# Partial softmax sums on VectorE in the first four attention units of a decoder layer

## The chip, the cores and the metric

The kernel runs on one NeuronCore of one Trainium2 chip, in fp32 throughout. The metric is the device time of one execution in microseconds. Five engines run side by side and are joined by semaphores: TensorE (PE; its weight loads are listed apart as PEld), VectorE (DVE), ScalarE (ACT), GpSimd (POOL) and the transfer queue of SyncE (SP). Matmul results go to PSUM banks of 128 partitions by 512 fp32 values.

## The reference, cut to what matters

A pre-norm decoder layer over 4 batches of 1024 tokens of width 512, with three residual blocks:

```
x = x + attn(layernorm(x))            # gated attention, 16 heads of 32
x = x + xattn(layernorm(x), ctx)      # cross attention, 16 heads of 32, 1024 context tokens
x = x + ffn(layernorm(x))             # 512 -> 64, 16 relu units for each of the 64, -> 512
```

The first attention divides twice, which is why two sums are needed:

```
attn_align = softmax(alignment)                                  # over keys
attn = attn_align * aperture[query] * expression[key]
attn = attn / (attn.sum(over keys) + 1e-8)
converged = attn @ v
```

With e = exp(score), the quotient needs the plain sum of e over the keys and the gated sum of e times expression[key], for each query and head. The cross attention needs the plain sum alone.

## The kernel before, in words

The work is cut into eight *units*: units 0 to 3 are the first attention of batches 0 to 3, units 4 to 7 the cross attention. A unit has two *halves* (512 queries each), a half has four *groups* of four heads, and a group runs over eight *key tiles* of 128 keys. One key tile of one group is a *step* (`attention`, `step`); there are 512. I call one group of one half of one unit a *group half*, written (unit, half, group).

A step does this:

- `scores` (L631): TensorE multiplies keys by queries for the four heads into two PSUM tiles `s`, each two banks wide. ScalarE turns each into a tile `e` of two heads by 512 queries (L637). There are six buffers of `e`, and a step takes two: `es[0]` holds the first two heads of the group, `es[1]` the third and fourth.
- Then VectorE adds. In units 0 to 3 it adds the first two heads up over the key tiles, plainly (L659 and L661, tile `es`) and with the gates (L668 on ScalarE begins it at key tile 1, L669 on VectorE goes on, tile `eg`).
- One step later, `times` (L684): TensorE multiplies `e` by the values into `av`. For the third and fourth heads it also makes the sums: after each odd key tile a *round* of four matmuls (L694) takes two key tiles times two heads; its weights are two columns of `sw`, a column of ones and the gates, so one matmul gives plain and gated sum, accumulated over the group in PSUM `sm`. A group half of units 0 to 3 has four such rounds.
- At the end of a group, `normalize` copies `av` and `sm` out (ScalarE, L703 and L705). One step on, after the scores of step 1 of the next group, `add_up` sums `es` and `eg` over the 128 partitions with matmuls by ones (L716), ScalarE copies the result (L717), small transfers rearrange the sums, and some steps later `divide` (L740 to L760) and `multiply` (L767) on VectorE apply the reciprocals to `q`, where `av` was put.

In units 4 to 6 VectorE adds all four heads. In the last unit the third and fourth heads of most groups go to TensorE by rounds of ones; there `added_up` names runs of three key tiles that VectorE adds up first.

Beside the steps, `run` deals out other work in proportion to its cost: projections of the next unit into two banks `f` (`bank`; L107), emptied by VectorE (`v` of units 0 to 3 L557, output projections L861) or ScalarE (L309, L311); layer norms on VectorE and GpSimd; the small feed-forward network of the previous half in units 5 to 7 (`hidden`, L1013 to L1024, in tiles `hid` with five buffers; `outputs`, L1035 and L1043). The order of work on every engine is the order in which the program issues it; nothing is reordered.

The output weights `wout` and output bias `bout_bc` of the network are constants that GpSimd's queue loads early (`load_networks` in unit 1, `load_biases` before unit 0). After the last step a hand-written tail (`go`) finishes the last half: the output products of the held half before it (`held_out`), transposes (`tr`), the network's inputs (`inputs`), hidden units and outputs.

Of the kernel before, what the change touches and what calls it, by code (L numbers as in the profile page):

```python
# [69 lines left out]
def moderate_path(tc: tile.TileContext, a: dict, out: bass.AP, flag: bass.AP):  # L70
    nc = tc.nc
    x = a["x"]
    with ExitStack() as st:
# [51 lines left out]
        make_identity(nc, ident)  # L125
        fixed = const.tile([P, 3], F32, name="fixed")
        ones, share, power = (fixed[:, i : i + 1] for i in range(3))
        for one, is_ in ((ones, 1.0), (power, -0.5), (share, 1.0 / M)):
            nc.gpsimd.memset(one, is_)

# [103 lines left out]
        bout_bc = const.tile([P, D], F32, name="bout_bc")  # L234

        def load_biases():

            nc.gpsimd.tensor_copy(bqk[:, 0, :], S[0]["rs"])
            for k in range(2):
                nc.gpsimd.dma_start(  # L240
                    bqk[k * 2 * DH : (k + 1) * 2 * DH], a["bqk"].rearrange("p w (c k) -> p w c k", k=2)[:, :, :, k]
                )
            nc.gpsimd.dma_start(bvT, a["xattn_bv"].rearrange("(c p) -> p c", p=P))
            nc.gpsimd.dma_start(bo_bc, a["xattn_bo"].partition_broadcast(P))
            nc.gpsimd.dma_start(bout_bc, a["ffn_bout"].partition_broadcast(P))
            by_quarters([nc.gpsimd.dma_start], win, a["ffn_Win"])

        def fold_bv(part=[]):
# [12 lines left out]


        win = const.tile([P, NC, M], F32, name="win")
        wout = const.tile([P, D], F32, name="wout")
        fb = const.tile([P, 4], F32, name="fb")
        units = const.tile([P, 4, INNER], F32, name="units")
        per = P // INNER

        def load_networks(k):
            r = slice(k * M, (k + 1) * M)  # L270
            nc.gpsimd.dma_start(wout[r, :], a["ffn_Wout"])
            nc.gpsimd.dma_start(fb[r, 0:2], a["ffb"])
            for c in range(NF):
                for w in range(3):
                    nc.gpsimd.dma_start(
                        units[k * M + c * per : k * M + (c + 1) * per, w, :],
                        a["units"].rearrange("(m h) w c -> c w m h", h=INNER)[c, w],
                    )
        def fold_bin():

            nc.vector.scalar_tensor_tensor(
                units[:, 1, :], units[:, 0, :], fb[:, 0:1], units[:, 1, :], ALU.mult, ALU.add
            )
            nc.vector.tensor_tensor(units[:, 3, :], units[:, 1, :], units[:, 2, :], ALU.mult)
            nc.vector.tensor_reduce(fb[:, 2:3], units[:, 3, :], AX.X, ALU.add)
            nc.vector.tensor_reduce(fb[:, 3:4], units[:, 3, 0:EARLY], AX.X, ALU.add)
            for i in (2, 3):
                nc.vector.tensor_tensor(fb[:, i : i + 1], fb[:, i : i + 1], fb[:, 1:2], ALU.add)
            nc.vector.tensor_scalar(units[:, 3, :], units[:, 1, :], -1.0, None, ALU.mult)
# [87 lines left out]
        def pre(u):  # L377
# [119 lines left out]
            def gates(hf):  # L497
                def f():

                    pg = bank()  # L500
                    for c in range(NC):
                        for t in range(4):
                            nc.tensor.matmul(  # L503
                                pg[t * 2 * H : (t + 1) * 2 * H, 0:P], lhsT=wae[:, c, :],
                                rhs=me["in", hf, "t"](c, t), start=(c == 0), stop=(c == NC - 1),
                            )

                    gi = p2.tile([P, 2 * P], F32, tag="hid", name="gi", bufs=5)[:, 0:P]
# [96 lines left out]
        def attention(u, hf):  # L605
# [6 lines left out]
            def shared(g):  # L612
                return ph == 0 or (u + 1 == len(order) and not (g == 1))

            added_up = {(0, 0): (0, 4), (0, 2): (0,), (0, HG - 1): (0, 4), (1, 0): (0, 4), (1, 2): (0,)} if u + 1 == len(order) else {}

            def apart(g):
                return 2 if u + 1 < len(order) else 3
# [1 line left out]
            def closing(g):  # L620
                return (u, hf, g) == (len(order) - 1, 1, HG - 1)

            def scores(g, kt):
# [38 lines left out]
                if ph == 0 and kt > 0:  # L662
                    if kt == 1:
                        me["eg"] = p1.tile([P, 2, HALF], F32, tag="es1", name="eg")
                    for h in range(2):
                        eg, gate = me["eg"][:, h, :], lambda t: me["sw"][:, t, HG * g + h, 1:2]
                        if kt == 1:
                            nc.scalar.activation(eg, me["e", 0][0][:, h, :], AF.Identity, scale=gate(0))  # L668
                        nc.vector.scalar_tensor_tensor(eg, es[0][:, h, :], gate(kt), eg, ALU.mult, ALU.add)  # L669
                return es  # L670

            def by_ones(tiles, first, last):
# [8 lines left out]
            def times(g, kt, es):  # L681
                for h in range(HG):
                    r = slice(h * DH, (h + 1) * DH)
                    nc.tensor.matmul(  # L684
                        av[r, :], lhsT=me["v"][:, kt, HG * g + h, :], rhs=es[h // 2][:, h % 2, :],
                        start=(kt == 0), stop=(kt == NT - 1),
                    )
                own = added_up.get((hf, g), ())
                if shared(g) and kt % 2 and kt - 1 not in own and not closing(g):

                    for j in range(4):
                        t, h = kt - 1 + j // 2, j % 2
                        rhs = me["es"][1] if t - 2 in own else me["e", t][1]
                        nc.tensor.matmul(  # L694
                            sm[j * DH : j * DH + sums, :],
                            lhsT=me["sw"][:, t, HG * g + 2 + h, :] if ph == 0 else ones, rhs=rhs[:, h, :],
                            start=(kt == (3 if 0 in own else 1)), stop=(kt == NT - 1),
                        )

            def normalize(g):  # L700
                i = (u * 2 + hf) * HG + g
# [115 lines left out]
        def post(u, hf):  # L817
# [76 lines left out]
                nc.vector.scalar_tensor_tensor(nm, res["mv"][:, 0:2, 0], -1.0, res["rs all"], ALU.mult, ALU.mult)  # L894

            def more_bias(t):
                return lambda: nc.gpsimd.tensor_tensor(res[t], res[t], bout_bc, ALU.add)

            def prepare():
                all_ = p2.tile([P, NC, T], F32, tag="k", name="rest")  # L900
# [34 lines left out]
                back(rows_d[b][hf], res["xn"])  # L935

            def biased(t):
                return lambda: nc.vector.tensor_tensor(res[t], res[t], bout_bc, ALU.add)

            def tr(t):  # L940
                def f():
# [63 lines left out]
            def hidden(h):  # L1005
                def f():
# [1 line left out]
                    part = (u, hf) == (n - 2, 0)  # L1008
                    own = u + 1 < n and (h < EARLY or not part)
                    if h < INNER:  # L1010
                        hid = p2.tile([P, 2 * P], F32, tag="hid", name="hid", bufs=5)
                    if own and h < INNER:
                        nc.vector.tensor_scalar(  # L1013
                            hid, res["s"], units[:, 0, h : h + 1], units[:, 3, h : h + 1], ALU.mult, ALU.max
# [16 lines left out]
            def outputs(t):  # L1031
                def products():
                    po = res["po", t] = [behind(), behind()] if u + 1 == n else [bank(), bank()]
                    for k in range(2):
                        nc.tensor.matmul(  # L1035
                            po[k], lhsT=res["g"][k * M : (k + 1) * M, ts(t, P)], rhs=wout[k * M : (k + 1) * M, :],
                            start=True, stop=True,
                        )
# [12 lines left out]
                return f, products, add  # L1051
# [64 lines left out]
        def one(f):  # L1116
            return [[(0, f)]]
# [13 lines left out]
        def beside(u, hf):  # L1131
# [768 lines left out]
```

## Time and profile before

| | |
|---|---|
| median of 3 runs | 2150.87 us (2150.67 to 2151.63) |
| profiled execution, its own time | 2150.95 us |
| its span, first to last instruction | 2149.2 us |
| granted TensorE clock | 0.999 |
| busy: TensorE, VectorE, ScalarE, GpSimd | 2132.1, 1529.4, 1234.8, 136.3 us |
| attention steps, first `av` to the tail | 103.7 to about 2112 us |
| units 0 to 3 | 103.7 to 1194.1 us |

How to read the rows: a row of the page's groups has line, engine, operation, output<-input by tile names, shapes, count, then busy time in us and mean length in ns, then the engine's idle time just before these instructions and what ended it. An fp32 matmul of the program shows as two records, so a round of four matmuls has eight. Matmuls overlap: the length of a record or run reaches into the next, and what a round takes of TensorE is read from start to start. A row of the timeline has start and length in us, then the same names; equal neighbours are merged, and brackets give the engine's idle time before and who ended it. A row of the windows has the stretch, its length, busy time of each engine with counts, the granted clock, the share of the transfer engines and GB/s.

### The profile page before, as it was taken

To read this page: it belongs to the slowest core of one execution; us is meant where nothing else is said; L and a number is where in the kernel's file an instruction comes from. 1 tells how busy PE (TensorE), PEld (TensorE's weight loads), DVE (VectorE), ACT (ScalarE), POOL (GpSimd) and SP (SyncE) were. 2 spreads that over 40 slices of the span, in tenths; PEclk is the share of its full clock that TensorE was granted. 3 is DMA by queue.
4 is the path that set the end of the run, shared out by engine and by line. 5 is a ranking of instruction groups with operands and counts; after the bars stand their busy time and mean duration, and the time that the engine had idled before them with its cause. 6 is when DMAs were issued, how large, how long until landed. Compare 5 with 4: busy or idle time off the path is not lost.

```text
span 2149.2 us, 52523 instructions
## 1 busy us (share of the span) xinstructions
PE 2132.1 (99%) x22556; PEld 549.5 (26%) x22556; DVE 1529.4 (71%) x2275; ACT 1234.8 (57%) x1499; POOL 136.3 (6%) x182
## 2 busy tenths in 40 slices
PE   9999999999999999999999999999999999999997
PEld 4322222222222222222222222222222222222223
DVE  3477575687666875657567576787778778788887
ACT  0156545655556554565656666565656656577774
POOL 2000010040030100001000010000000000000001
PEclk9999999999999999999999999999999999999999
DMA  6412133132341312212322213231433223232231
GB/s 165 129 47 56 65 99 111 21 90 72 81 117 31 86 39 71 71 42 72 67 74 74 67 46 70 77 104 47 109 86 80 78 54 71 71 90 71 71 91 50
DMA packets 154496, 161.81 MB, mean 75 GB/s; under 512 B 47366, under 2 KB 93062, under 8 KB 153100
## 3 DMA queue, kind: packets, MB, share of 16 engines
q1 hardware_dynamic: 150188, 156.26, 26.2%
q8 instruction: 179, 2.93, 0.6%
q0 software_dynamic: 2080, 0.98, 0.3%
q10 hardware_dynamic: 1984, 1.12, 0.2%
q14 instruction: 65, 0.53, 0.1%
HBM read 115.53 MB, written 42.73 MB: 74 GB/s over the span
## 4 chain that ended last, share of the span: by engine, by line
PE 96%; DVE 2%; ACT 1%; issue 1%; DMA 0%; POOL 0%; SPq 0%; DVEq 0%; POOLq 0%; ACTq 0%
PE f L107 37%; PE s L631 24%; PE av L684 22%; PE sm L694 6%; PE sm L716 3%; PE f L960 1%; ACT e L637 1%; PE s L107 1%; DVE es L661 1%; PE f L631 1%; PE f L1035 0%; DVE res L1043 0%; DMA xin<-in_x 0%; PE f L503 0%; PE f L994 0%
## 5 line engine op out<-in xcount | busy, mean ns | idle before, releaser
L637 ACT ACTIVATE e<-s 128x1024 f32<-128x1024 f32 x999 | 971.4, 1023 | 704.6 <-PE s L631 495.0
L661 DVE TENSOR_TENSOR es<-es,e 128x1024 f32<-128x1024 f32 x542 | 650.0, 1224 | 244.3 <-ACT e L637 243.2
L631 PE MATMUL s<-q,k 32*64 32x512 f32 x7992 | 585.9, 613 | 0.4 <-ACT e L637 0.2
L684 PE MATMUL av<-e,v 128*32 128x512 f32 x4096 | 548.0, 603 | 0.0
L107 PE MATMUL f<-xT,w 128*32 128x512 f32 x2816 | 333.7, 592 | 0.0
L669 DVE SCALAR_TENSOR_TENSOR eg<-e,sw,eg 128x512 f32<-128x512 f32 x448 | 315.3, 745 | 9.0 <-ACT eg L668 9.0
L659 DVE TENSOR_TENSOR es<-e 128x1024 f32<-128x1024 f32 x97 | 115.9, 1222 | 209.8 <-ACT e L637 199.4
L107 PE MATMUL f<-w,q 128*32 128x512 f32 x1984 | 238.3, 592 | 1.8 <-DVE q L767 1.7
L631 PEld LDWEIGHTS s<-q,k 32*64 32x64 f32 x7992 | 127.7, 129 | 413.8 <-ACT e L637 203.3
L684 PEld LDWEIGHTS av<-e,v 128*32 128x32 f32 x4096 | 87.6, 108 | 403.1 <-issue 402.8
L107 PEld LDWEIGHTS f<-xT,w 128*32 128x32 f32 x2816 | 92.0, 110 | 210.6 <-issue 207.6
L694 PE MATMUL sm<-e,sw 128*2 128x512 f32 x1024 | 133.3, 592 | 0.0
L107 PE MATMUL f<-w,xT 128*32 128x512 f32 x896 | 106.0, 592 | 0.6 <-DVE q L313 0.6
L107 PEld LDWEIGHTS f<-w,q 128*32 128x32 f32 x1984 | 64.3, 110 | 152.4 <-issue 143.0
L107 PE MATMUL f<-w,ctxT 128*32 128x512 f32 x768 | 92.3, 592 | 0.0
L107 PE MATMUL f<-ctxT,w 128*32 128x512 f32 x768 | 92.3, 592 | 0.0
L869 POOL TENSOR_TENSOR r<-res,bo_bc 128x512 f32<-128x512 f32 x32 | 40.9, 1280 | 760.2 <-DVE res L861 634.6
L716 PE MATMUL sm<-es,fixed 128*1 128x512 f32 x356 | 65.0, 591 | 0.0
L319 POOL TENSOR_SCALAR rs<-fmv 128x4 f32<-128x4 f32 (+2 forms) x18 | 11.8, 657 | 835.8 <-DVE fmv L866 835.5
L861 DVE TENSOR_TENSOR res<-f,res 128x512 f32<-128x512 f32 x62 | 42.4, 684 | 19.6 <-PE f L107 12.1
L1024 DVE SCALAR_TENSOR_TENSOR g<-hid,units,g 128x256 f32<-128x256 f32 x105 | 50.1, 477 | 2.7 <-ACT hid L1017 1.9
L767 DVE TENSOR_TENSOR q<-q,recb 128x512 f32<-128x512 f32 x63 | 43.0, 683 | 6.3 <-DMA recb<-rec_d 6.2
(283 smaller groups left out, 1167.1 us busy)
## 6 DMA issues: line engine op xcount, KB each, us to landing
recb<-rec_d SPq DMA_DIRECT2D x252, 64.0 KB
xT<-rows_d SPq DMA_DIRECT2D x60, 256.0 KB
rows_d<-r SPq DMA_DIRECT2D x60, 256.0 KB
w<-in_xattn_Wo SPq DMA_DIRECT2D x9, 1024.0 KB
w<-wout_d SPq DMA_DIRECT2D x8, 1024.0 KB
res<-in_x SPq DMA_DIRECT2D x32, 256.0 KB
x1b_d<-r SPq DMA_DIRECT2D x32, 256.0 KB
res<-x1b_d SPq DMA_DIRECT2D x32, 256.0 KB
```

Source lines behind the costliest of these rows:

```text
L107: nc.tensor.matmul(to[r], lhsT=lhsT[:, j, :] if len(lhsT.shape) == 3 else lhsT[:, r], rhs=rhs, **flags)
L631: nc.tensor.matmul(two[j][m : m + 64], lhsT=k[r, g, kt * P + m : kt * P + m + 64], rhs=q[r, g, :], start=True, stop=True,)
L637: nc.scalar.activation(e[:, h, :] if len(reads) == 1 else e[:, h.start, :], s, AF.Exp, scale=SCALE)
L659: nc.vector.tensor_tensor(me["es"][i], me["e", begin][i], es[i], ALU.add)
L661: nc.vector.tensor_tensor(me["es"][i], me["es"][i], es[i], ALU.add)
L669: nc.vector.scalar_tensor_tensor(eg, es[0][:, h, :], gate(kt), eg, ALU.mult, ALU.add)
L684: nc.tensor.matmul(av[r, :], lhsT=me["v"][:, kt, HG * g + h, :], rhs=es[h // 2][:, h % 2, :], start=(kt == 0), stop=(kt == NT - 1),)
L694: nc.tensor.matmul(sm[j * DH : j * DH + sums, :], lhsT=me["sw"][:, t, HG * g + 2 + h, :] if ph == 0 else ones, rhs=rhs[:, h, :], start=(kt ...
L716: nc.tensor.matmul(sm[j * DH : j * DH + 1, :], lhsT=ones, rhs=e, start=True, stop=True)
L767: nc.vector.tensor_tensor(own, own, all_, ALU.mult)
L861: nc.vector.tensor_tensor(r, res["po"], r, ALU.add)
L1024: nc.vector.scalar_tensor_tensor(res["g"], res["hid"], units[:, 2, h - 1 : h], res["g"], ALU.mult, ALU.add)
```

## The change

In 19 of the 32 group halves of units 0 to 3, VectorE adds up the third and fourth heads over the first m key tiles (m is 4 or 6), plainly into a tile `ep` and with the gates into a tile `et`. ScalarE begins `et` at key tile 1. TensorE's rounds for these key tiles are left out (two or three of four), and one round comes instead, after key tile 6 (m=4) or 7 (m=6), whose four matmuls sum the two heads of `ep` and of `et` over the partitions; `pick` puts the plain sums in the first and the gated sums in the second row. Group halves with m=4: (0,1,0), (0,1,1), (0,1,2), (1,0,0), (1,1,0), (1,1,1), (1,1,2), (2,0,0), (2,1,1), (2,1,2), (3,0,0), (3,0,3), (3,1,0), (3,1,1), (3,1,3). With m=6: (0,1,3), (1,1,3), (2,1,0), (2,1,3).

Room for the two tiles (one buffer each) is made by the constants of the network's output and by `hid`: weights and bias are now loaded in unit 4 into the place of `ep`, and four `hid` buffers are a ring in the place of `et`. The gates get two buffers of their own. In the last unit, (7,1,0) has one run of three key tiles added up in place of two. In the tail, the two output products of the held half stand ahead of the transposes.

```diff
+        pick = const.tile([P, 3], F32, name="pick")
+        nc.gpsimd.memset(pick, 0.0)
+        nc.gpsimd.memset(pick[:, 1:2], 1.0)
...
-            nc.gpsimd.dma_start(bout_bc, a["ffn_bout"].partition_broadcast(P))
...
-            nc.gpsimd.dma_start(wout[r, :], a["ffn_Wout"])
...
+        def load_outs():
+            both = p1.tile([P, 2, HALF], F32, tag="exa", name="outs")
+            outs["w"], outs["b"] = both[:, 0, :], both[:, 1, :]
+            for k in range(2):
+                nc.gpsimd.dma_start(outs["w"][k * M : (k + 1) * M, :], a["ffn_Wout"])
+            nc.gpsimd.dma_start(outs["b"], a["ffn_bout"].partition_broadcast(P))
...
-                    gi = p2.tile([P, 2 * P], F32, tag="hid", name="gi", bufs=5)[:, 0:P]
+                    gi = p2.tile([P, P], F32, tag="gi", name="gi")
...
-            added_up = {(0, 0): (0, 4), (0, 2): (0,), (0, HG - 1): (0, 4), (1, 0): (0, 4), (1, 2): (0,)} if u + 1 == len(order) else {}
+            added_up = {(0, 0): (0, 4), (0, 2): (0,), (0, HG - 1): (0, 4), (1, 0): (0,), (1, 2): (0,)} if u + 1 == len(order) else {}
+
+            gated = {(0, 1, 0): 4, (0, 1, 1): 4, (0, 1, 2): 4, (0, 1, 3): 6, (1, 0, 0): 4, (1, 1, 0): 4, (1, 1, 1): 4, (1, 1, 2): 4, (1, 1, 3): 6, (2, 0, 0): 4, (2, 1, 0): 6, (2, 1, 1): 4, (2, 1, 2): 4, (2, 1, 3): 6, (3, 0, 0): 4, (3, 0, 3): 4, (3, 1, 0): 4, (3, 1, 1): 4, (3, 1, 3): 4}
...
+                m = gated.get((u, hf, g), 0)
+                if 0 < kt < m:
+                    gate = lambda t, h: me["sw"][:, t, HG * g + 2 + h, 1:2]
+                    if kt == 1:
+                        me["ep"], me["et"] = (p1.tile([P, 2, HALF], F32, tag=k, name=k) for k in ("exa", "exb"))
+                        nc.vector.tensor_tensor(me["ep"], me["e", 0][1], es[1], ALU.add)
+                    else:
+                        nc.vector.tensor_tensor(me["ep"], me["ep"], es[1], ALU.add)
+                    for h in range(2):
+                        et = me["et"][:, h, :]
+                        if kt == 1:
+                            nc.scalar.activation(et, me["e", 0][1][:, h, :], AF.Identity, scale=gate(0, h))
+                        nc.vector.scalar_tensor_tensor(et, es[1][:, h, :], gate(kt, h), et, ALU.mult, ALU.add)
...
-                if shared(g) and kt % 2 and kt - 1 not in own and not closing(g):
...
+                if not shared(g) or closing(g):
+                    return
+                own, m = added_up.get((hf, g), ()), gated.get((u, hf, g), 0)
+
+                def round_(seats, start, stop):
+                    for j, (lhsT, rhs) in enumerate(seats):
+                        nc.tensor.matmul(sm[j * DH : j * DH + sums, :], lhsT=lhsT, rhs=rhs, start=start, stop=stop)
+
+                if kt % 2 and kt - 1 not in own and kt >= m:
+                    seats = []
                     for j in range(4):
                         t, h = kt - 1 + j // 2, j % 2
                         rhs = me["es"][1] if t - 2 in own else me["e", t][1]
...
+                        seats.append((me["sw"][:, t, HG * g + 2 + h, :] if ph == 0 else ones, rhs[:, h, :]))
+                    round_(seats, kt == (3 if 0 in own else max(m + 1, 1)), kt == NT - 1 and m < 6)
+                if m and kt == min(m + 2, NT - 1):
+                    seats = [(pick[:, 1 - w : 3 - w], me["et" if w else "ep"][:, h, :]) for w in range(2) for h in range(2)]
+                    round_(seats, False, m == 6)
...
-                        hid = p2.tile([P, 2 * P], F32, tag="hid", name="hid", bufs=5)
+                        if "ring" not in S:
+                            S["ring"], S["turn"] = p1.tile([P, 4, 2 * P], F32, tag="exb", name="ring"), 0
+                        hid = S["ring"][:, S["turn"] % 4, :]
+                        S["turn"] += 1
...
-                return out + k[1] + xT[0] + v[1][0:2] + tr[0]
+                return out + k[1] + xT[0] + v[1][0:2] + (one(load_outs) if u == B else []) + tr[0]
...
-        go(norm[2], bias[2], o[7], lambda: root(3, 1), *tr[0:3], held_out[0][1], look, lambda: within(0, most), norm[3])
-        go(bias[3], *bias[0:2], tr[3], held_out[0][2], lambda: inputs(((0, 0, 2), (1, 2, 1))), held_out[1][1])
-        go(lambda: inputs(((1, 3, 1),)), held_out[1][2], lambda: within(most, most + 1))
+        go(norm[2], bias[2], o[7], lambda: root(3, 1), held_out[0][1], held_out[1][1], *tr[0:3], look, lambda: within(0, most))
+        go(norm[3], bias[3], *bias[0:2], tr[3], held_out[0][2], lambda: inputs(((0, 0, 2), (1, 2, 1))))
+        go(lambda: inputs(((1, 3, 1),)), held_out[1][2], lambda: within(most, most + 1))
```

More of the change, by code (lines that the diff above doesn't have):

```diff
@@ L233, in moderate_path @@
         bo_bc = const.tile([P, D], F32, name="bo_bc")
-        bout_bc = const.tile([P, D], F32, name="bout_bc")
+        outs = {}
         def load_biases():
@@ L263, in moderate_path @@
         win = const.tile([P, NC, M], F32, name="win")
-        wout = const.tile([P, D], F32, name="wout")
         fb = const.tile([P, 4], F32, name="fb")
@@ L687, in times @@
                     )
-                own = added_up.get((hf, g), ())
-                if shared(g) and kt % 2 and kt - 1 not in own and not closing(g):
+                if not shared(g) or closing(g):
[6 more added lines that the diff above has]
+                    seats = []
                     for j in range(4):
@@ L693, in times @@
                         rhs = me["es"][1] if t - 2 in own else me["e", t][1]
[L694 to L698, printed above, removed]
+                        seats.append((me["sw"][:, t, HG * g + 2 + h, :] if ph == 0 else ones, rhs[:, h, :]))
[3 more added lines that the diff above has]
+                    round_(seats, False, m == 6)
             def normalize(g):
@@ L896, in more_bias @@
             def more_bias(t):
-                return lambda: nc.gpsimd.tensor_tensor(res[t], res[t], bout_bc, ALU.add)
+                return lambda: nc.gpsimd.tensor_tensor(res[t], res[t], outs["b"], ALU.add)
             def prepare():
@@ L937, in biased @@
             def biased(t):
-                return lambda: nc.vector.tensor_tensor(res[t], res[t], bout_bc, ALU.add)
+                return lambda: nc.vector.tensor_tensor(res[t], res[t], outs["b"], ALU.add)
             def tr(t):
@@ L1035, in products @@
                         nc.tensor.matmul(
-                            po[k], lhsT=res["g"][k * M : (k + 1) * M, ts(t, P)], rhs=wout[k * M : (k + 1) * M, :],
+                            po[k], lhsT=res["g"][k * M : (k + 1) * M, ts(t, P)], rhs=outs["w"][k * M : (k + 1) * M, :],
                             start=True, stop=True,
```

## The prediction

> **What bounds the kernel now.** I name a group half (u, h, g): unit u, query half h, head group g; each has eight steps, one per key tile. I read first the busy shares and the chain on the page, then the cost of each line, then the timeline of one group half, then windows over the 19 group halves that the change touches.
>
> The page's busy times, the chain by engine, and the lines whose work is moved:
>
> ```profile
> PE 2132.1 (99%) x22556; PEld 549.5 (26%) x22556; DVE 1529.4 (71%) x2275; ACT 1234.8 (57%) x1499; POOL 136.3 (6%) x182
> PE 96%; DVE 2%; ACT 1%; issue 1%; DMA 0%; POOL 0%; SPq 0%; DVEq 0%; POOLq 0%; ACTq 0%
> L661 DVE TENSOR_TENSOR es<-es,e 128x1024 f32<-128x1024 f32 x542 | 650.0, 1224 | 244.3 <-ACT e L637 243.2
> L631 PE MATMUL s<-q,k 32*64 32x512 f32 x7992 | 585.9, 613 | 0.4 <-ACT e L637 0.2
> L669 DVE SCALAR_TENSOR_TENSOR eg<-e,sw,eg 128x512 f32<-128x512 f32 x448 | 315.3, 745 | 9.0 <-ACT eg L668 9.0
> L694 PE MATMUL sm<-e,sw 128*2 128x512 f32 x1024 | 133.3, 592 | 0.0
> ```
>
> TensorE never waits here: 0.4 us ahead of all the score matmuls, 0.0 ahead of the sum matmuls. VectorE waits 243 us for exponentials. So the time is the length of TensorE's stream, as long as nobody makes it wait.
>
> The timeline of group half (0,1,3), start and length in us:
>
> ```profile
> 344.37 1.11 PE L631 MATMUL s<-q,k 32*64 32x512 f32 x16
> 345.42 1.07 PE L684 MATMUL av<-e,v 128*32 128x512 f32 x8
> 346.30 1.04 PE L694 MATMUL sm<-e,sw 128*2 128x512 f32 x8
> 346.58 1.23 DVE L661 TENSOR_TENSOR es<-es,e 128x1024 f32<-128x1024 f32 x1 [1.60 <-ACT e L637]
> 347.16 2.76 PE L107 MATMUL f<-xT,w 128*32 128x512 f32 x24
> 352.11 1.22 DVE L661 TENSOR_TENSOR es<-es,e 128x1024 f32<-128x1024 f32 x1 [1.04 <-ACT e L637]
> 353.25 1.41 DVE L669 SCALAR_TENSOR_TENSOR eg<-e,sw,eg 128x512 f32<-128x512 f32 x2
> 361.34 1.22 DVE L661 TENSOR_TENSOR es<-es,e 128x1024 f32<-128x1024 f32 x1 [2.97 <-ACT e L637]
> 371.71 1.41 DVE L669 SCALAR_TENSOR_TENSOR eg<-e,sw,eg 128x512 f32<-128x512 f32 x2
> 377.74 0.60 PE L716 MATMUL sm<-eg,fixed 128*1 128x512 f32 x2
> ```
>
> Two things are to be seen. A round of four sum matmuls (8 records) takes TensorE from 346.30 to 347.16: 0.86 us; the 1.04 is its length with the overlap into the next round. And VectorE's wide add occupies it from 352.11 to 353.25, 1.14 us, though its length is 1.22; a pair of gated adds takes 1.33 by the same reading (316.38 to 317.71 in the timeline further up).
>
> Windows over the two fullest group halves and the sum over all 19 (length, then busy PE, PEld, DVE, ACT, POOL):
>
> ```profile
> 341.70:378.60 36.90, 36.90 (x391) 9.11 (x387) 21.93 (x32) 21.03 (x27) 0.23 (x1) 1.00 0.56 153
> 618.50:655.40 36.90, 36.90 (x388) 9.11 (x384) 22.77 (x39) 21.02 (x27) 0.23 (x1) 1.00 0.56 153
> sum 677.60, PE 677.60 PEld 167.47 DVE 423.70 ACT 381.04 POOL 39.88; mean PE 35.66 PEld 8.81 DVE 22.30 ACT 20.05 POOL 2.10
> ```
>
> TensorE is busy all the time in them; VectorE has 254 us free.
>
> **The change part by part.**
>
> *TensorE loses rounds.* With m key tiles added up first, m/2 rounds go and one round on the sums comes: 15 group halves with m=4 lose one, 4 with m=6 lose two: 23 rounds, 23 x 0.86 = 19.8 us. The new round has the same shape (two-column weights, 512 columns), so the same price. This lies wholly on the path.
>
> *VectorE gains adds.* Each of m-1 key tiles costs 1.14 + 1.33 = 2.47 us by starts; 15x3 + 4x5 = 65 key tiles are 160.6 us against 254 us free. The slowest rows bound it: a wide add beside GpSimd's took 1.45, and with two gated adds of 0.75 that is 2.95. I take 2.47, the undisturbed row. [...]
>
> Who waits behind these adds? (a) The sum of the gated first two heads, read by the ones-matmuls (L716) in step 1 of the next group. In (0,1,3) VectorE waits 1.60, 0.83, 1.04, 1.16, 2.97, 0.56 and 0.57 us between its first and last add: 8.73 us of cover for 5 x 2.47 = 12.35. The last gated add, which ends at 373.12, ends 3.62 later, at 376.74. Its reader, at 377.72, stands 1.72 earlier (three rounds gone, one come), at 376.00: TensorE waits 0.74, with hand-over some 0.9. (1,1,3) has the same gaps within 0.1: 0.9 again. The same sum over the other seventeen, with what is carried in, leaves the reader 1.1 us or more, least in (2,0,0). (b) Exponentials three steps later need the buffer of e (six buffers, two a step). The smallest margin is 0.2 us, at key tile 3 of (2,0,0), and ScalarE may be 1.7 us late there before scores wait. (c) VectorE's emptying of projection banks (L557, L861): the next use of the bank comes 6 to 7 us after it in these halves, the adds push it by up to 6, and 1.3 us stay. (d) The new round itself runs two steps or more after the last add it reads: 2.5 us or more stay. So (a) costs 1.8; between 0 (if the order of adds lets the gated sum through earlier) and 8 (at 2.95 a key tile, which adds 2.4 in each of the four six-tile halves and uses up their margins).
>
> *ScalarE gains* 38 scalings at 0.72, 27 us; it has some 16 us free in each group half. Its next exponential starts about 1.4 us later in the short steps of (1,0,0) and (2,0,0) (3.7 us a step), where the second score bank then comes free some 0.2 late: 0.5 in all, between 0 and 1.
>
> *The last unit.* In (7,1,0) the second run of three is no longer added up: VectorE loses two wide adds, TensorE gains one round (+0.86). There stands TensorE's longest wait outside start and tail:
>
> ```profile
> 2028.12 2.35 DVE L661 TENSOR_TENSOR es<-es,e 128x1024 f32<-128x1024 f32 x2
> 2031.83 0.69 DVE L767 TENSOR_TENSOR q<-q,recb 128x512 f32<-128x512 f32 x1
> 2032.57 1.06 PE L107 MATMUL f<-w,q 128*32 128x512 f32 x8 [1.67 <-DVE q L767]
> ```
>
> With 2 x 1.14 = 2.3 off VectorE ahead of L767 and a round put in ahead of the reader, the 1.67 goes: -0.8 net; between +0.86 (if the reciprocals' transfer lands just then) and -0.8.
>
> *The tail.* Both output products of the held half move ahead of the transposes; the second, 0.86 of TensorE, no longer stands at 2129.99 between the rounds that feed the last hidden layer. But the transposes start about 2 us later (the second product waits for L861, which ends at 2124.86), and their banks then hold the inputs up by 0.4. I take -0.5, between -0.9 (the round alone) and +1.0 (if the bank of the third transpose comes later still).
>
> *Costed at nothing:* the output weights and bias are loaded in unit 4 by GpSimd (landing 4.8 and 6.2 us, first read in unit 5; if late, unit 5's biases wait that long, 6 us); they move past GpSimd's root computations, ahead of which it idles for 835 us in all. The tiles that hold them, the new sums and the ring of four are written long after their former readers in TensorE's order. The ring lets ScalarE run one unit less ahead in the tail; VectorE is 0.57 us a unit there and ScalarE 0.51, so it stays hidden (0 to 0.5). The gates' own two buffers are read within their unit.
>
> *Sum:* -19.8 + 1.8 + 0.5 - 0.8 - 0.5 = -18.8. The profiled execution took 2150.95 us (span 2149.2, 1.75 around it), 0.08 from the median 2150.87: 2132.2 us.
>
> **The rivals.**
>
> 1. *Cover runs out in the six-tile halves and a few more.* At 2.95 us a key tile the 8 us under (a) are lost: 2138 us, and up to 2146 if (b) and (c) bind too in the halves with margins below 1.5. For it: margins of 0.2 to 1.3. Against: undisturbed adds keep 1.14 all along the timeline.
>
> 2. *Slower: VectorE fills the 19 halves.* Its place is the adds' queue, through the buffers of e. They hold 677.6 - 19.8 = 657.8 us; VectorE needs 423.7 + 65p. It is full at p = 3.6 us, the gain is gone at p = 3.9, and at p = 4.2 the time is 2150.95 + 19.1 - 1.3 = 2169 us. For it: the wide add rose to 1.45 beside GpSimd. Against: that is 1.2 times, and 1.6 is needed; and in the last unit VectorE is busy 85% while TensorE waits under 2 us.
>
> 3. *TensorE's stream is not the bound.* Its records overlap, so 99% could hide a pace set elsewhere; dropped rounds would then leave no trace: about 2150 us. Against: the steps with a sum round are longer by just that round, 0.86. [...]
>
> **How the numbers follow.** Forecast as summed 0.76; rival 1, 0.14; rival 3, 0.03; rival 2, 0.07. The low end is everything hidden: -19.8 - 0.8 - 0.9 = -21.5, 2129.5. The high end is 2140, rival 1's first figure and a little more; about 0.17 stay outside (rivals 2 and 3, and the upper half of rival 1). No change means within 0.2% (4.3 us), about what a measurement can tell. Faster 0.9, same 0.03, slower 0.07.
>
> **What would show it.** Sum matmuls of TensorE fewer by 88 (176 records); the group half (0,1,0) shorter by 0.86, (2,1,0) by 1.72; VectorE some 170 us busier in units 0 to 3, ScalarE 27; waits of TensorE for VectorE of about 1 us at the ends of (0,1,3) and (1,1,3) alone; no 1.67 wait in (7,1,0). Wrong it is if the 19 halves aren't shorter, if TensorE's waits in them come to over 8 us, or if ScalarE's exponentials wait for VectorE's release of e.

## The result and the profile after

The changed kernel takes 2135.4 us (median of 6 runs, 2134.35 to 2137.01) against 2150.86 us before (6 runs, 2150.67 to 2152.69): ratio 0.9926, 95% interval 0.9916 to 0.9936. The forecast was 2132.2 us, the range 2129.5 to 2140.0. The gain is 15.5 us instead of 18.7.

The execution that was profiled after the change took 2137.01 us, with a span of 2135.2 us, so it is the slowest of the six; its span is 14.0 us shorter than that of the profile before. Lines of that profile: busy time of each engine, the rows that answer to those shown of before, and the rows of the new round (line, engine, operation, output<-input, shapes, count, then busy us, mean ns, idle us before it and what ended it). The profile calls the tile `ep` `exa` and the tile `et` `exb`; `both` is the copy of a group's sums. Line numbers move by a few from kernel to kernel.

```profile
PE 2118.0 (99%) x22380; PEld 551.5 (26%) x22380; DVE 1677.9 (79%) x2468; ACT 1255.8 (59%) x1537; POOL 139.3 (7%) x184
L671 DVE TENSOR_TENSOR es<-es,e 128x1024 f32<-128x1024 f32 x541 | 649.7, 1226 | 123.2 <-ACT e L647 121.9
L641 PE MATMUL s<-q,k 32*64 32x512 f32 x7992 | 589.3, 613 | 0.5 <-ACT e L647 0.2
L107 PE MATMUL f<-xT,w 128*32 128x512 f32 x2816 | 333.7, 592 | 0.7 <-DVE xT L347 0.7
L679 DVE SCALAR_TENSOR_TENSOR eg<-e,sw,eg 128x512 f32<-128x512 f32 x448 | 315.2, 744 | 9.0 <-ACT eg L678 9.0
L692 DVE SCALAR_TENSOR_TENSOR exb<-e,sw,exb 128x512 f32<-128x512 f32 x130 | 91.4, 743 | 0.0
L717 PE MATMUL sm<-e,sw 128*2 128x512 f32 x688 | 89.5, 592 | 0.0
L717 PE MATMUL sm<-exa,pick 128*2 128x512 f32 x76 | 19.5, 592 | 0.0
L717 PE MATMUL sm<-exb,pick 128*2 128x512 f32 x76 | 19.5, 592 | 0.0
```

TensorE has 176 records fewer, as forecast, and 14.1 us less to do. VectorE has 148 us more, and its idle time ahead of the wide adds (L671, before L661) has halved from 244 to 123 us. Between the first key tile and the tail, the only new wait of TensorE over 0.2 us is 0.7 us for the transposed blocks (L347).

The chain that ended last can be followed back only to 928 us in this profile, so its shares can't be compared with those of before. Windows over (0,1,3), (1,1,3) and the sum over all 19 group halves of the changed kernel:

```profile
342.36:378.08 35.72, 35.38 (x372) 8.58 (x368) 33.57 (x47) 22.11 (x29) 0.22 (x1) 1.00 0.55 158
615.22:650.95 35.73, 35.39 (x373) 8.59 (x369) 34.42 (x54) 22.12 (x29) 0.22 (x1) 1.00 0.56 157
sum 662.73, PE 662.00 PEld 163.93 DVE 574.43 ACT 402.32 POOL 42.03; mean PE 34.84 PEld 8.63 DVE 30.23 ACT 21.17 POOL 2.21
```

The 19 halves take 662.7 us, from first `av` to first `av`, and took 677.8: 15.1 us less, where 19.8 (the rounds alone) or 17.5 (with the forecast's two losses) were expected. TensorE is still busy in all but 0.7 us of them. So most of what is missing is not waiting: some runs of matmuls take longer.

Where the 14.0 us of the span come from, stage by stage, by the starts of the key tiles in the two traces:

| stage | forecast, us | trace, us |
|---|---|---|
| 23 rounds less | -19.8 | -19.8 (exact in 12 of 19 halves) |
| VectorE late in (0,1,3), (1,1,3) | +1.8 | +1.1 |
| short steps of (1,0,0), (2,0,0), (3,0,0), (3,0,3), (3,1,0) | +0.5 | +3.6 |
| (7,1,0) | -0.8 | -1.0 |
| tail, from the last key tile on | -0.5 | -1.7 |
| start, up to the first key tile | 0 | +3.2 |
| (6,1,1), (6,1,2) | 0 | +0.6 |
| sum | -18.8 | -14.0 |

The row of (6,1,1) and (6,1,2) is no part of the change: it is 0.0 in six of the traces below, among them all four whose start is early (experiments 2, 7 with the adds alone, 9 and 10), and between 0.3 and 1.1 in the others. Its cause is open.

### The profile page after: what moved, and what is told of

It reads as the page before. It is cut to its first block, busy times and chain, and to the rows that moved or that the text cites. A ratio compares the mean times of both kernels' runs of the same rounds, so it can differ in the third digit from the quotient of the medians.

```text
span 2135.2 us, 52477 instructions
## 1 busy us (share of the span) xinstructions
PE 2118.0 (99%) x22380; PEld 551.5 (26%) x22380; DVE 1677.9 (79%) x2468; ACT 1255.8 (59%) x1537; POOL 139.3 (7%) x184
## 4 chain that ended last, share of the span: by engine, by line
PE 55%; DVE 1%; issue 0%; ACT 0%; DVEq 0%; ACTq 0%
PE f L107 19%; PE s L641 15%; PE av L707 14%; PE sm L746 2%; PE sm L717 2%; PE f L990 1%; PE f L641 1%; PE f L1068 0%; PE s L107 0%; DVE res L1076 0%; PE f L1024 0%; DVE es L671 0%; ACT e L647 0%; PE s L1068 0%; PE sm L697 0%
## 5 line engine op out<-in xcount | busy, mean ns | idle before, releaser
L671 DVE TENSOR_TENSOR es<-es,e 128x1024 f32<-128x1024 f32 x541 | 649.7, 1226 | 123.2 <-ACT e L647 121.9
L692 DVE SCALAR_TENSOR_TENSOR exb<-e,sw,exb 128x512 f32<-128x512 f32 x130 | 91.4, 743 | 0.0
L717 PE MATMUL sm<-e,sw 128*2 128x512 f32 x688 | 89.5, 592 | 0.0
L746 PE MATMUL sm<-es,fixed 128*1 128x512 f32 x356 | 65.3, 591 | 0.0
L687 DVE TENSOR_TENSOR exa<-exa,e 128x1024 f32<-128x1024 f32 x46 | 55.9, 1216 | 0.0
```

The lines of the kernel that those rows point to most:

```text
L671: nc.vector.tensor_tensor(me["es"][i], me["es"][i], es[i], ALU.add)
L687: nc.vector.tensor_tensor(me["ep"], me["ep"], es[1], ALU.add)
L692: nc.vector.scalar_tensor_tensor(et, es[1][:, h, :], gate(kt, h), et, ALU.mult, ALU.add)
L717: nc.tensor.matmul(sm[j * DH : j * DH + sums, :], lhsT=lhsT, rhs=rhs, start=start, stop=stop)
L746: nc.tensor.matmul(sm[j * DH : j * DH + 1, :], lhsT=ones, rhs=e, start=True, stop=True)
```

## The experiments

In all of them the time is a median beside that of the kernel before on the same chip (2151.1 to 2151.5 us). Runs of one kernel differ by 1 to 5 us here, so single halves are judged by the traces, in which the length of nearly every half repeats within 0.01 us.

**1. Who begins the gated sums.** In five halves VectorE does it instead of ScalarE.

```
+ if (u, hf, g) in ((1, 0, 0), (2, 0, 0), (3, 0, 0), (3, 0, 3), (3, 1, 0)):
+     nc.vector.tensor_scalar(et, me["e", 0][1][:, h, :], gate(0, h), None, ALU.mult)
+ else:
      nc.scalar.activation(et, me["e", 0][1][:, h, :], AF.Identity, scale=gate(0, h))
```

> In the five halves (1,0,0), (2,0,0), (3,0,0), (3,0,3) and (3,1,0) the two gated sums are begun by VectorE (a multiplication by the gate) instead of ScalarE. Theory: ScalarE's two scalings of 0.7 us stand ahead of the exponentials of the next key tile and lengthen step 2 there (0.42 us in (1,0,0) and (2,0,0), about 1.0 in (3,0,0) and 0.9 in (3,1,0)). Then these steps shorten and the five halves together lose 2.2 to 2.9 us; the 0.22 us of step 4 stay. Rival: VectorE's adds, through the buffers of e, are what is late; with two operations more on VectorE the five halves stay as they are or grow by up to 2 us. Whole time 2132.5 to 2133.5 by the theory, 2135 to 2138 by the rival.

Measured: 2133.45 us (2131.98 to 2134.49), ratio 0.9917 (0.9903 to 0.9931). The five halves give back 2.71 us: 0.42, 0.42, 0.79, 0.15 and 0.93. Step 2 of (1,0,0) in the changed kernel, ScalarE and TensorE (timeline rows: start, length, names):

```profile
379.82 0.72 ACT L678 ACTIVATE eg<-e,sw 128x512 f32<-128x512 f32 x1
380.44 1.33 ACT L691 ACTIVATE exb<-e,sw 128x512 f32<-128x512 f32 x2
381.66 0.57 ACT L747 COPY both<-sm 128x512 f32<-128x512 f32 x1
382.13 1.95 ACT L647 ACTIVATE e<-s 128x1024 f32<-128x1024 f32 x2
383.69 1.53 PE L641 MATMUL s<-q,k 32*64 32x512 f32 x16
```

and in this experiment:

```profile
378.58 0.72 ACT L678 ACTIVATE eg<-e,sw 128x512 f32<-128x512 f32 x1
379.19 0.58 ACT L750 COPY both<-sm 128x512 f32<-128x512 f32 x1
379.83 1.94 ACT L647 ACTIVATE e<-s 128x1024 f32<-128x1024 f32 x2
381.19 0.48 DVE L692 TENSOR_SCALAR exb<-e,sw 128x512 f32<-128x512 f32 x1
...
382.44 1.11 PE L641 MATMUL s<-q,k 32*64 32x512 f32 x16
```

With ScalarE's two scalings (L691) ahead of them, the exponentials begin 2.31 us after the scaling of `eg` instead of 1.25. The scores of the next step then take 1.53 instead of 1.11 us, because the second score bank comes free late: the matmuls into it start at 384.13 us, 0.05 us after the second exponential (382.13 + 1.95) has ended. No wait is written for this: the matmuls only look longer. VectorE's own way to begin costs 0.48 us a head. The theory holds; VectorE was not what was late here.

**2. No rounds dropped.**

```
- gated = {(0, 1, 0): 4, ..., (3, 1, 3): 4}
+ gated = {}
```

> All of the change but the added-up third and fourth heads: no group half is in the list. Theory: the 19 halves give 15.1 us in the changed kernel and all of this comes back, while (7,1,0) keeps its -1.0 and the tail its -1.8 against the kernel before: 2148 us, 2150.5 if the start stays late by 3 us as in the changed kernel's trace. Rival: part of the 15 us is shifted from or to another place (start, tail, last unit); then those places differ from the changed kernel's by as much.

Measured: 2148.26 us (2147.72 to 2149.55), ratio 0.9987 (0.9978 to 0.9996). All 19 halves are back to 0.00; (7,1,0) keeps -1.0 and the tail -1.7: leaving out the first part of the change doesn't alter what the two others give. But the start is early again (first key tile at 104.0 us, 106.9 in the changed kernel), though the instructions up to there are the same: see experiments 8 to 10.

**3. Four key tiles instead of six** in two halves.

```
- (0, 1, 3): 6, ... (1, 1, 3): 6
+ (0, 1, 3): 4, ... (1, 1, 3): 4
```

> (0,1,3) and (1,1,3) add up four key tiles instead of six. One more round each: +0.86. Theory: VectorE's lag at the end of these halves makes TensorE wait 0.55 each for the transposed blocks; with 2 key tiles fewer (5 us of VectorE) that wait goes, so net +0.3 a half, +0.6 in all. Rival: the wait does not come from the adds (the blocks' transfer is late anyway): +0.86 a half, +1.7 in all. Whole time 2136 or 2137.

Measured: 2136.04 us (2135.01 to 2137.24). Each of the two halves is 0.31 us longer, and TensorE's wait of 0.7 us is gone: the theory's figure. The end of (0,1,3) in the changed kernel, TensorE and VectorE:

```profile
371.79 2.48 DVE L347 STREAM_TRANSPOSE xT<-xT 128x512 f32<-128x512 f32 x4
372.96 0.60 PE L717 MATMUL sm<-exb,pick 128*2 128x512 f32 x2
...
374.33 1.92 PE L107 MATMUL f<-xT,w 128*32 128x512 f32 x16 [0.34 <-DVE xT L347]
...
375.30 1.40 DVE L679 SCALAR_TENSOR_TENSOR eg<-e,sw,eg 128x512 f32<-128x512 f32 x2
377.23 0.60 PE L746 MATMUL sm<-es,fixed 128*1 128x512 f32 x2
```

VectorE is late, as the prediction said, but the first to feel it is the projection that reads the transposed blocks (L347, queued behind the adds), not the ones-matmuls (L746), which then come in time.

**4. Two halves left out** that lost by the change.

```
- (3, 0, 0): 4, ... (3, 1, 0): 4,
```

> (3,0,0) and (3,1,0) add up nothing. Theory: in them the change costs more than its round (+0.15 and +0.29 in the trace), and without it they are back at the lengths of the kernel before: -0.44 us. Rival: the round's 0.86 is merely paid elsewhere in the neighbouring halves, and taking it out returns +1.7 over the unit. Whole time 2135 by the theory, 2137 by the rival.

Measured: 2135.27 us (2134.15 to 2136.36). By the trace the 19 halves give 15.51 instead of 15.06 us, both halves are back at 0.00 and no neighbour moves.

**5. The plain add made twice.**

```
  nc.vector.tensor_tensor(me["ep"], me["ep"], es[1], ALU.add)
+ nc.vector.tensor_tensor(me["ep"], me["ep"], es[1], ALU.add)
```

> Each wide plain add of the third and fourth heads is made twice in the 19 halves, 65 adds of 1.14 us more on VectorE (their plain sums count the added key tiles twice, so the output is another). A key tile then costs 3.6 us, the price at which the prediction's second rival has VectorE full in these halves. Theory (the cover is used half by half, and steps of 4.7 us hold 6.4 us of VectorE's work while keys are added up): the lag passes what the six buffers of e and the banks allow in the halves with short steps and in the six-tile halves, TensorE waits 10 to 30 us in all, and most of the gain is gone: 2145 to 2165 us. Rival (there is far more cover than the halves' sums say, since VectorE catches up in the steps without adds): under 5 us, 2136 to 2140.

Measured: 2181.05 us (2178.78 to 2183.97), ratio 1.014 (1.0125 to 1.0156): slower than before the change by 30 us, more than either side expected. TensorE's waits in units 0 to 3 (what for: us, times, longest):

```profile
PE f L107 <- DVE xT L347: 8.9, 2, 4.4
PE f L107 <- DVE v L565: 5.8, 3, 2.6
PE sm L718 <- DVE exa L688: 2.8, 4, 0.7
PE f L107 <- DVE res L892: 2.6, 3, 0.9
PE s L641 <- ACT e L647: 1.6, 3, 1.2
```

The 19 halves grow by 43.2 us against the changed kernel: 21.5 are waits, the rest is matmuls that take longer (busy 683.7 instead of 662.0 us), some behind late exponentials and some at half clock. The half clock is the smaller share: the mean granted clock is 0.996 here and 0.998 in the changed kernel, by which I estimate some 4 us over the whole span (0.002 x 2178; 2 to 7 with the rounding). One stretch of it, about 3.4 us, follows the longest wait (4.45 us, granted clock 0.62 from 384 to 388 us and 0.95 from 388 to 392). ScalarE's exponentials, on the other hand, now wait for VectorE's adds to release their buffers of `e` (ScalarE's waits in units 0 to 3):

```profile
ACT e L647 <- DVE eg L679: 27.3, 21, 1.9
ACT e L647 <- DVE exb L693: 21.5, 17, 2.7
ACT e L647 <- DVE exa L688: 8.1, 4, 2.2
```

So the cover ends between 2.5 us a key tile, where the change stands, and 3.6.

**6. Tail and last unit undone.**

```
- (1, 0): (0,), (1, 2): (0,)
+ (1, 0): (0, 4), (1, 2): (0,)
- go(..., root(3, 1), held_out[0][1], held_out[1][1], *tr[0:3], look, ...)
+ go(..., root(3, 1), *tr[0:3], held_out[0][1], look, ...)    # the order before, in both lines
```

> The order of the tail and the second run of three in (7,1,0) are as in the kernel before; the rest of the change stays. The prediction's sizes give +0.5 for the tail and +0.8 for (7,1,0), 1.3 us; the traces of before and after give +1.8 and +1.0, 2.8 us. Whole time 2136.7 or 2138.2. Rival for the tail: the 1.8 come from elsewhere (another landing time, the ring); then the tail stays at 35.6 us from the last key tile instead of 37.3.

Measured: 2141.16 us (2137.78 to 2142.73), ratio 0.9949 (0.9936 to 0.9963). The tail is back at 37.4 us from the last key tile (35.6 changed, 37.3 before): the 1.7 us are the order's. (7,1,0) however is 3.0 us longer than in the changed kernel, not 1.0: VectorE's L797 comes 0.35 later than before, TensorE waits 2.0 instead of 1.7, and then this (windows: length, busy time of each engine, granted clock third from the end):

```profile
2019.00:2021.00 2.00, 0.00 (x1) 0.00 (x1) 2.00 (x6) 0.11 (x1) 0.00 (x0) 1.00 0.00 0
2021.00:2022.00 1.00, 1.00 (x8) 0.15 (x8) 1.00 (x1) 0.00 (x0) 0.00 (x0) 0.58 0.00 0
2022.00:2023.00 1.00, 1.00 (x12) 0.25 (x16) 0.93 (x4) 0.00 (x0) 0.00 (x0) 0.50 0.00 0
2024.00:2025.00 1.00, 1.00 (x12) 0.16 (x8) 0.96 (x4) 0.14 (x1) 0.00 (x0) 0.71 0.00 0
```

The clock is granted at half from 2021.16 to 2024.58 us (where 0.58 and 0.71 put the edges), and costs about another 1.6 us (an estimate: 3.0 less 1.0 and less the 0.35). The wait of 1.67 before the change had no such sequel: the clock is 1.00 from 2031 to 2036 us there.

**7. Rounds and adds apart.** First the adds alone (TensorE keeps its old rounds), then the rounds alone.

```
- own, m = added_up.get((hf, g), ()), gated.get((u, hf, g), 0)      # adds alone, in times
+ own, m = added_up.get((hf, g), ()), 0
```

```
- m = gated.get((u, hf, g), 0)                                       # rounds alone, in scores
+ m = 0
- seats = [(pick[:, 1 - w : 3 - w], me["et" if w else "ep"][:, h, :]) ...]
+ seats = [(pick[:, 1 - w : 3 - w], es[1][:, h, :]) ...]
```

> VectorE and ScalarE do all the adds of the 19 halves, but TensorE keeps its rounds of the kernel before and reads none of the new sums. Theory (the adds cost TensorE nothing where its own steps are longer, and the 4.7 us lost of the 19.8 appear only once the rounds are gone): the 19 halves change by 0.0 to +0.3 us, all of it in (3,0,0) and (3,1,0); 2148.3 to 2148.6 us with the start of the kernel without rounds dropped. If the late start (first key tile at 105 to 107 instead of 104 us) belongs to the VectorE instructions of the 19 halves, it shows here: 2150 us. Rival (the adds themselves slow TensorE, by buffers or by the ports of the memory): the 19 halves grow by about 4.7 us.

> TensorE drops the 23 rounds as in the change, but nothing is added up: the rounds on the sums read the exponentials of the key tile at hand instead, so the sums of the third and fourth heads leave key tiles out. Theory: without VectorE's and ScalarE's new work the waits for transposed blocks and for late exponentials go, and only the floor of the steps (scores, exponentials, score banks) stays, 0.22 us each in (1,0,0), (2,0,0), (3,0,0) and (3,1,0): the 19 halves give 18.9 us, 2129.4 us in all, or 2131.5 with the late start. Rival (the losses are TensorE's own, by the order of its rounds): they give 15 to 16 us as in the changed kernel.

Measured: adds alone 2150.41 us (2150.05 to 2151.39), 19 halves +1.67 us, neither the 0.3 of the theory nor the 4.7 of the rival: +0.54 in (1,0,0) and (2,0,0), +0.45 in (3,1,0), +0.15 in (3,0,0), 0.00 in the other fifteen. Of this, 1.0 us is the old round's own wait for ScalarE's copy of the sums of the group before, which stands behind the scalings; the rest shows as no wait (TensorE's waits in units 0 to 3):

```profile
PE sm L717 <- ACT both L747: 1.0, 3, 0.4
```

The first key tile starts at 103.4 us here, so VectorE's new instructions don't bring the late start.

Rounds alone: 2133.97 us (2131.72 to 2134.53), 19 halves -18.84 us, the theory's 18.9. What is left of 19.78 is 0.22 to 0.23 in each of four halves: their step 4 (step 2 in (3,0,0)) takes 3.12 us, where the old length without the round would be 2.90, with or without adds. The scores in it take 1.34 us instead of 1.11 (at 390.76 us in the changed kernel), and again the matmuls into the second score bank start late, at 391.01 us, 0.05 us after the exponential that empties it. So it looks like the pace of scores, exponentials and score banks, which no run here changed by itself.

**8. x ahead of the weights.**

```
  for t in range(4):
-     if t == 2:
-         by_quarters(queues, wk0, W_IN["k0"][0])
      queues[t % 2](x0[:, t, :], x[0, t * P : (t + 1) * P, :])
+ by_quarters(queues, wk0, W_IN["k0"][0])
```

> The first weights' transfer is issued after all four tiles of x instead of after two. Theory: the first tile of x lands late in the changed kernel (5.5 us instead of 4.3) because the weights' packets share the transfer engines with it, TensorE runs dry for 1.3 us, and the clock is granted at half for 3.4 us after. With x alone the first normalization starts at 4.3 us or earlier, the clock stays at 1.00 and the time falls by 1.5 to 3 us: 2132.5 to 2134. Rival: the first tile, which is issued ahead of the weights in both kernels, is late for another reason; then it lands at 5.5 us or later as before and the time stays at 2135.4, or grows by as much as the weights come later.

Measured: 2135.95 us (2135.3 to 2136.97). The first tile is there at 4.53 us, yet nothing is gained: the weights are later, TensorE is busy 0.13 of the 2 us from 8 to 10, the clock is halved from about 11.4 us on, and the first key tile starts at 105.3.

**9. One half only.**

```
+ gated = {(0, 1, 0): 4}
```

> Of the 19 halves only (0,1,0) adds up. Theory (the start depends on the program as a whole, not on what stands at its start): with one half the start is as in the kernel with none, first key tile at 104.0 us and clock 0.999, and the time is 2148.3 - 0.9 = 2147.4 us. Rival (the new tiles and the adds as such, even once, bring the late start): first key tile at 105.7 us or later, clock 0.998 in most runs, 2149 us. (0,1,0) is shorter by 0.86 either way.

Measured: 2147.6 us (2147.14 to 2148.54); first key tile at 103.6 us, and (0,1,0) is 0.86 us shorter. The rival falls: neither the new tiles nor the adds of one half bring the late start. That doesn't show yet what does.

**10. TensorE's program made long again** by 92 matmuls of one column after the last products.

```
  go(products, final[0][0], final[1][0])
+ more = bank()
+ for _ in range(92):
+     nc.tensor.matmul(more[0:1, 0:1], lhsT=least, rhs=ones, start=True, stop=True)
```

> 92 matmuls of one column are put behind the last output products, so that TensorE's program is again as long as in the kernel before (22564 records instead of 22380); nothing else differs from the changed kernel. So far the first tile of x was there at 4.0 to 4.3 us and the first key tile began at 103.4 to 104.0 us in the kernels with 22556 or more records of TensorE, and at 4.5 to 6.8 and 105.3 to 107.7 us in those with 22396 or fewer, though the instructions up to there are the same. Theory (the start goes with the length of TensorE's program, whatever is in it): x is there at 4.3 us or earlier, the first key tile begins at 104.0 us or earlier, and the clock is 0.999 in every run. Rival (it goes with what the dropped rounds do, or is chance): first key tile at 105 us or later and a clock of 0.997 or 0.998 in most runs. The whole time grows by up to 11 us for the matmuls themselves at the end, whatever the start does.

Measured: 2135.57 us (2134.93 to 2136.41), though the end grew by 1.7 us. The start, in the profile of the changed kernel and then in this one (timeline: first normalization of x and first transposes of it):

```profile
5.54 0.69 DVE L430 BATCH_NORM_STATS2 bnst<-xin 128x6 f32<-128x512 f32 x1 [3.60 <-DMA xin<-in_x]
8.05 1.08 PE L354 MATMUL f<-ident,xin 128*32 128x128 f32 x32 [1.33 <-DVE xin L332]
10.00 3.54 PE L107 MATMUL s<-xin,w 128*32 128x128 f32 x64 [0.86 <-ACT xin L360]
```

```profile
4.11 0.69 DVE L430 BATCH_NORM_STATS2 bnst<-xin 128x6 f32<-128x512 f32 x1 [2.17 <-DMA xin<-in_x]
6.63 1.08 PE L354 MATMUL f<-ident,xin 128*32 128x128 f32 x32
9.25 1.95 PE L107 MATMUL s<-xin,w 128*32 128x128 f32 x64 [1.54 <-DMA w<-in_attn_Wo]
```

The same 64 matmuls take 3.54 us in the changed kernel, where the granted clock is 0.50 from 10 to 12 us, and 1.95 here, as in the kernel before, where it is 1.00. The first key tile starts at 103.8 us and not at 106.9, and the mean clock is 0.998 to 0.999, not 0.999 in every run. So in this profile the beginning comes earlier with what is added at the very end of TensorE's program, and the length fits all fourteen profiles (five with 22556 records or more: first key tile at 103.4 to 104.0; nine with 22396 or fewer: 105.3 to 107.7). There is one profile of each kernel, and only this experiment lengthens the program without bringing rounds back, so chance isn't excluded. (The chip isn't the reason: on three chips early and late starts were measured side by side.) Without the 1.7 us at the end the median would be 1.6 us below the changed kernel's, about half of what the two starts differ by. What the length does to the transfer, whose issue times are the same within 0.01 us (but for experiment 8), stays open; no run shows it.

**11. Experiment 1 with one more half in the list.**

```
- (3, 0, 0): 4, (3, 0, 3): 4
+ (3, 0, 0): 4, (3, 0, 1): 4, (3, 0, 3): 4      # VectorE begins the gated sums in (3, 0, 1) too
```

> VectorE begins the gated sums in the five halves as in the first experiment, and (3,0,1), in which VectorE has 9.3 us free there, adds up four key tiles as well (3 x 2.5 us and two scalings). Theory: another 0.64 to 0.86 us, 2132.6 to 2132.8 us. Rival: VectorE runs late in (3,0,1) or in the halves after it, and the time stays at 2133.5 or grows.

Measured: 2133.24 us (2130.27 to 2134.55), ratio 0.9912 (0.9898 to 0.9925). (3,0,1) is 0.86 us shorter and no other half of units 0 to 3 changes against experiment 1. The median moved by only 0.2, which says nothing beside runs that differ by up to 4.3 us; in its profile the start is later than in experiment 1's (107.7 instead of 105.7 us). By the traces, the halves of units 0 to 3 take 3.6 us less than in the changed kernel; the whole times, whose intervals overlap, don't show it as clearly.

## Why the prediction was right, and where it was off

- *TensorE's stream is the bound; a round is 0.86 us.* Right to 0.01 us: -0.86 or -1.72 in twelve halves, -18.84 with the rounds alone. Rival 3 falls: the dropped rounds left their trace, and the time fell by 15.5 us while VectorE's share rose from 71% to 79%.
- *2.47 us of VectorE a key tile.* Right by starts: the new adds start 1.14 us (plain) and 1.32 us (gated pair) apart, still less than their lengths of 1.22 and 1.41. VectorE's busy time in the 19 halves rose by 150.7 us, less than 65 x 2.47 = 160.6 and than the 170 named as a sign; why wasn't followed up.
- *(a), VectorE late at the end of (0,1,3) and (1,1,3):* right place, wrong reader, size 0.55 instead of 0.9 each. The step that failed is the list of who waits behind the adds: it went from the last gated add to its own reader and skipped the transposes queued between. In the six-tile half (2,1,3) nothing is lost, so this is not the number of adds alone.
- *ScalarE, 0.5 us:* the mis-sized term. With (a) it makes 4.7 us instead of 2.3. The trace's sum misses the forecast's by 4.8 us: 2.4 for these two, 3.8 for the start and (6,1,1) and (6,1,2), less 1.4 by which the last unit and the tail gave more than forecast. The median missed by only 3.2, since the profiled execution was the slowest of the six; and without the 1.4, which is luck, either miss would be larger. Scalings and their followers cost 2.7 us (experiment 1), the floor of the short steps 0.9 (rounds alone). The prediction followed late exponentials through (1,0,0) and (2,0,0) alone and left out (3,0,0) and (3,1,0), whose steps are as short and which lost most; and it had no floor, since step 4 never stood without its round in the old trace.
- *Last unit and tail:* direction right, -1.0 and -1.7 instead of -0.8 and -0.5. In the tail the inputs did start 0.6 us later after the last key tile, as forecast, but then run through: they end 1.2 us earlier, without the second product in between. The wait of 0.9 us ahead of the one small matmul of L1249 is gone, but in its place TensorE waits 1.0 us for the first hidden unit (L1024), so little is gained by that.
- *What was costed at nothing:* loads, tiles, the buffers of `e`, the emptied banks and the new round itself, rightly: none of them makes TensorE wait for over 0.2 us. One sign of being wrong did come, in small: in units 0 to 3 ScalarE's exponentials wait four times for VectorE's adds to release `e`, in (3,0,0), (3,0,3) and (3,1,1), and never before the change (waits of ScalarE: total us, times, longest). The steps they fall in are no longer for it.

```profile
ACT e L647 <- DVE exa L687: 1.6, 2, 1.2
ACT e L647 <- DVE eg L679: 0.8, 2, 0.4
```

- *The start* was not in the sum at all; it took 3.2 us in the profiled execution.
- *Rival 1 and 2:* the price of 2.95 us wasn't met. Experiment 5 shows that rival 2's point was far too generous. At 3.6 us a key tile it had VectorE just full and the gain still whole; in fact the kernel is then 30 us slower than before. Averages over 19 halves hide that VectorE must be in time in each; the place is the adds' queue, as rival 2 said. The waits that the profile writes for TensorE stand at the transposes, `v`, the emptied banks and the rounds on the new sums, only 1.6 us of them at exponentials; but the buffers of `e` are in it too, since ScalarE waits 57 us for VectorE to release them and about half of the loss is matmuls that only look longer.

## What to carry to other kernels

Where one engine's stream is the bound, count what leaves it at its start-to-start price, and then look for the loss not in its waits alone but in steps whose matmuls take longer: late exponentials showed up here as stretched score matmuls (1.53 instead of 1.11 us). Ahead of each added operation ask who is queued behind it on that engine, in the shortest step, one half at a time; a sum over all halves tells only that it could fit. Small helper operations belong on the engine that isn't feeding the bound one just then: two scalings on ScalarE stretched a step by 0.15 to 0.93 us, and the same two on VectorE by nothing, though VectorE had the less free time of the two.

## What the runs showed of the hardware that was not expected

- In fourteen profiles, one of each kernel, the first transfer lands at 3.98 to 4.31 us where TensorE's program has 22556 records or more, in one of them by matmuls after the last product, and at 4.53 to 6.82 us where it has 22396 or fewer. In six of the nine late ones (the changed kernel, experiments 1, 3, 4, 6 and 8) the windows show the clock halved for 3.4 or 6.8 us, beginning at 8.0 to 11.4 us; in the early ones of the kernel before and of experiments 2 and 9 it stands at 1.00 up to 30 us. In the late ones the first key tile starts 1.3 to 4.3 us later. The cause is open.
- After a wait of 2.0 us in experiment 6 the granted clock was halved for 3.4 us; in the 3.4 us ahead of the drop TensorE was busy for 1.4. At the start of the changed kernel, the granted clock of 0.97 from 8 to 10 us and 0.68 from 12 to 14 puts the slow stretch at 9.88 to 13.28 us, and TensorE was busy for 1.3 of the 3.4 us ahead of it; its longest single wait there was 1.33 us, shorter than the 1.67 us that had no sequel before the change. In the 3.4 us up to the end of that wait (2029.17 to 2032.57) TensorE was busy for 1.7, and the clock stayed at 1.00. So the length of the wait alone doesn't tell these three places apart; what brings a drop is not shown.
